# Attention over gathered neighbours: values without ones columns, one 512-column sum for both batches, and the softmax weights summed apart

## The chip, the cores and the metric

The kernel runs on one core of one Trainium2 chip. The metric is the device time in microseconds (us) of one execution. A core has five engines with queues of their own: TensorE (PE; its weight loads are shown apart as PEld), VectorE (DVE), ScalarE (ACT), GpSimd (POOL) and SyncE (SP). [...]

## The reference

Two layers over x, 8 batches of 2048 nodes with 256 features. Layer 0 is a graph convolution with two linear layers and batch norms. Layer 1, which the change concerns, is attention of each node over its neighbours in the graph, with 4 heads of 64. Both end in a residual sum and a layer norm:

```python
x = _layernorm(x + _L0_gnn_ref(x, adj, ...), axis=-1)
qkv = h @ W                                   # h is x; 256 -> 3 * 256
mask = jnp.where(adj == 0, -jnp.inf, 0.0)
scores = jnp.einsum('bhid,bhjd->bhij', q, k) / np.sqrt(HEAD_DIM) + mask
attn = jax.nn.softmax(scores, axis=-1)
out = jnp.einsum('bhij,bhjd->bhid', attn, v)
x = _layernorm(x + out, axis=-1)
```

The graph is sparse. The first nodes have many neighbours, later ones few.

## The kernel before

Layer 0 takes the first part of the span; the change leaves it as it is. Layer 1 is the function attention(). It works on pairs of batches (G2 = 2; four pairs, called passes here) and on 16 blocks of 128 nodes.

*Projection.* For each of the 8 units of a pair (a batch, and a stretch of 512 nodes) the kernel loads, norms and transposes the input and then forms keys, values and queries for 4 tiles of 128 nodes (keys_values, took_keys_values, queries, took_rows). Keys and values of a node go as one row of kv_d to DRAM, queries to q_d. A row of kv_d has 256 key columns and, for each head, 64 value columns and one column of ones, KW = 516 columns for each batch. The ones are there so that the weighted sum of a head's 65 columns gives the sum of the weights in the last one; a memset on GpSimd writes them, four at the start of each unit. Keys and values leave PSUM by two ScalarE copies (L1000, L1001).

*Block 0*, whose nodes have many neighbours, is done densely beside the projection: scores0, exps0, and weigh, which sums probabilities times the 65 columns of each head into po0 in PSUM.

*Blocks 1 to 15* use lists of neighbours. A block has ELL tiles, in which each node has its next neighbour, and CAP tiles of leftovers, in which 128 neighbours of any nodes of the block stand together. There are 132 tiles in a pass (92 and 40), 528 in all. Each tile n goes through: gather (GpSimd, L1165: 128 rows of kv_d into kg; for leftovers also query rows, L1171), score (VectorE: product pr, L1181, and its sum by heads, L1183), exps (ScalarE, L1192: the weights pw, 8 numbers a node), weigh_values (wv: values and ones times the weights, 520 columns; on VectorE, L1212, or in 8 pieces on ScalarE, L1207; for leftovers VectorE also makes the one-hot matrix oh that says which node each row belongs to, L1198), and add_up (TensorE, L1223: adds wv into the block's sum po, with the identity or with oh as the stationary operand; 260 columns, once for each batch of the pair).

The order is written out by hand. In step n of the loop stand score(n+5), exps(n+4), weigh_values(n+3), add_up of tile n-1 for the second batch and of tile n for the first, gather(n+10), then a slot of the next pair's projection (in the last pass there is none), then what was put off to this step: finish (reciprocal L1070 and product z L1072) one step after a block's last tile for the first batch and two for the second, residual (GpSimd, L1079), out_stats and later the output's norm and store.

Buffers tie the engines together: kg 10, wv 5, pw 4, pr 2, and in PSUM three banks for po (one for each batch of a block, so that a new block begins before the last one is finished), one for po0 and four for the rest. All eight banks are used.

```python
po[p, t, b] = ps_o.tile([P, NHEADS, VW], F32, name="po")
nc.tensor.matmul(
    po[p, t, b].rearrange("p h e -> p (h e)"), oh[n] if e >= 0 else ident,
    wv[n][:, b, :], start=(r == 0), stop=(r == ELL[t] + CAP[t] - 1),
)
```

Of the kernel before, what the change touches and what calls it, by code (L numbers as in the profile page):

```python
# [8 lines left out]
F32 = mybir.dt.float32  # L9
# [29 lines left out]
def tile_gcn_then_masked_attention(  # L39
# [803 lines left out]
    VW = HD + 1  # L843
    KW = D + NHEADS * VW
    inv_all = mpool.tile([P, B, NT, NHEADS], F32, name="inv_all")
# [45 lines left out]
    def attention():  # L891

        with ExitStack() as st:
            enter = st.enter_context
            ip = enter(tc.tile_pool(name="attn_in", bufs=2, side="left", reuse_waits="tile"))
            ps_o = enter(tc.tile_pool(name="ps_o", bufs=3, space=PSUM, reuse_waits="tile"))
            ps_z = enter(tc.tile_pool(name="ps_z", bufs=1, space=PSUM, reuse_waits="tile"))
            ps_m = enter(tc.tile_pool(name="ps_m", bufs=4, space=PSUM, reuse_waits="tile"))
            enter(tc.manual_schedule(engines=ALL4))

            x1, yt, x1t, ln, lo, kvr, qr, kt, q0, s0, p0, po0, zs, pms = ({} for _ in range(14))

# [58 lines left out]
            def first_queries(b):  # L961

                pm = pms["q0", b] = ps_m.tile([P, HP, P], F32, name="pm")
                for hp in range(HP):
                    for d in range(ND):
                        nc.tensor.matmul(
                            pm[:, hp, :], wq[:, d, hp * P : (hp + 1) * P], x1t[b, 0][:, d, :P],
                            start=(d == 0), stop=(d == ND - 1),
                        )
                q0[b] = ip.tile([P, HP, 2, P], F32, name="q0")  # L970
                for r in range(2):
                    nc.gpsimd.memset(q0[b][(1 - r) * HD : (2 - r) * HD, :, r, :], 0.0)
# [7 lines left out]
            def product(b, c, i, n, rhs):  # L980
# [6 lines left out]
                return pm  # L987

            def keys_values(b, c, i):
                if not i:  # L990
                    kvr[b, c] = ip.tile([P, TPC, KW], F32, name="kvr")
                    qr[b, c] = ip.tile([P, TPC, D], F32, name="qr")
                    for j in range(TPC):
                        nc.gpsimd.memset(heads(kvr[b, c][:, j, D:])[:, :, HD:], 1.0)
                pms["kv", b, c, i] = product(b, c, i, 2 * D, lambda d: wq[:, d, D:])

            def took_keys_values(b, c, i):
                pm = pms.pop(("kv", b, c, i))
                kv = kvr[b, c][:, i, :]
                nc.scalar.copy(kv[:, :D], pm[:, :D])  # L1000
                nc.scalar.copy(heads(kv[:, D:])[:, :, :HD], heads(pm[:, D:]))  # L1001

# [42 lines left out]
            def weigh(b, c, i):  # L1045
                j = c * TPC + i
                if not j:
                    po0[b] = ps_z.tile([P, NHEADS, VW], F32, name="po0")
                p = p0.pop((b, c, i))
                for h in range(NHEADS):  # L1050
                    nc.tensor.matmul(  # L1051
                        po0[b][:, h, :], p[:, h, :], heads(kvr[b, c][:, i, D:])[:, h, :],
                        start=(j == 0 and h == 0), stop=(j == NT - 1), skip_group_check=True,
                    )
# [12 lines left out]

            def finish(b, t, po):
                ri = inv_all[:, b, t, :]
                nc.vector.reciprocal(ri, po[:, :, HD])  # L1070
                z = zs[b, t] = ip.tile([P, D], F32, name="z", bufs=4)
                nc.vector.tensor_mul(  # L1072
                    heads(z), po[:, :, :HD], ri[:, :, None].to_broadcast([P, NHEADS, HD])
                )
# [24 lines left out]
            def projection(p, step):  # L1099
# [7 lines left out]
                for k, (b, c) in enumerate(units):  # L1107
# [26 lines left out]
                    if c == NCH - 1:  # L1134
                        at(u + 8, lambda b=b: finish(b, 0, po0.pop(b)))
                        at(u + 9, residual, b, 0)
                        at(u + 11, out_stats, b, 0)
# [12 lines left out]
            ON_ACT, LAST_ON_ACT = (1, 3), (0, 2, 4)  # L1150
            kg, qg, qb, oh, sc, pw, wv, po = ({} for _ in range(8))

# [23 lines left out]
            def score(n):  # L1176
                p, g = divmod(n, NG)
                t, r, col, e = tiles[g]
                q = qb[p, t] if e < 0 else qg.pop(n)
                pr = ep.tile([P, G2, D], F32, name="pr")  # L1180
                nc.vector.tensor_mul(pr, q, kg[n][:, :, :D])  # L1181
# [5 lines left out]
                sc[n] = s  # L1187

            def exps(n):
                col = tiles[n % NG][2]  # L1190
                pw[n] = ep.tile([P, G2, NHEADS], F32, name="pw", bufs=4)
                nc.scalar.activation(pw[n], sc.pop(n), AF.Exp, bias=padb[:, col : col + 1])  # L1192

            def weigh_values(n):
                e = tiles[n % NG][3]
                if e >= 0:
# [3 lines left out]
                    )  # L1200
                wv[n] = ep.tile([P, G2, NHEADS * VW], F32, name="wv", bufs=5)
                k, w = kg.pop(n), pw.pop(n)
                if n % 5 in (LAST_ON_ACT if n >= (NP - 1) * NG else ON_ACT):
                    for b in range(G2):
                        for h in range(NHEADS):
                            hs = slice(h * VW, (h + 1) * VW)
                            nc.scalar.activation(  # L1207
                                wv[n][:, b, hs], k[:, b, D:][:, hs], AF.Copy,
                                scale=w[:, b, h : h + 1],
                            )  # L1210
                    return
                nc.vector.tensor_mul(  # L1212
                    wv[n].rearrange("p b (h e) -> p b h e", e=VW),
                    k[:, :, D:].rearrange("p b (h e) -> p b h e", e=VW),
                    w[:, :, :, None].to_broadcast([P, G2, NHEADS, VW]),
                )

            def add_up(n, b):
                p, g = divmod(n, NG)
                t, r, col, e = tiles[g]  # L1220
                if not r:
                    po[p, t, b] = ps_o.tile([P, NHEADS, VW], F32, name="po")
                nc.tensor.matmul(  # L1223
                    po[p, t, b].rearrange("p h e -> p (h e)"), oh[n] if e >= 0 else ident,
                    wv[n][:, b, :], start=(r == 0), stop=(r == ELL[t] + CAP[t] - 1),
                )
                if b:
                    del wv[n]
                    oh.pop(n, None)

            def finish_block(p, t, b):
                finish(p * G2 + b, t, po.pop((p, t, b)))

# [15 lines left out]
            for n in range(NALL_G):  # L1249
# [10 lines left out]
                if n:  # L1260
                    add_up(n - 1, 1)
                add_up(n, 0)
                if n + LEAD < NALL_G:
# [3 lines left out]
                for f, args in later.pop(n, ()):  # L1267
                    f(*args)
                if r == ELL[t] + CAP[t] - 1:
                    for b in range(G2):  # L1270
                        u = n + 1 + b
                        at(u, finish_block, p, t, b)
                        at(u + 1, residual, p * G2 + b, t)
                        at(u + 3, out_stats, p * G2 + b, t)
                        if t % TPC == TPC - 1:
                            u = n + 5 + 2 * b
                            at(u, out_root, p * G2 + b, t // TPC)
# [3 lines left out]
                assert g < NG - 1 or not slots  # L1281
            add_up(NALL_G - 1, 1)
            for n in sorted(later):
# [373 lines left out]
```

## Time and profile before

| | |
|---|---|
| Median of 3 runs | 2501.35 us (2494.38 to 2505.6) |
| The profiled execution | 2506.55 us, span 2504.7 us |
| TensorE busy (8 thousand matmul records) | 2136.0 us, 85% |
| VectorE busy | 1892.7 us, 76% |
| ScalarE busy | 1248.2 us, 50% |
| GpSimd busy | 1467.8 us, 59% |
| DMA | 690.01 MB, mean 275 GB/s |
| Attention | from 1002 us to the end |

"L1223" is line 1223 of the kernel. A shape such as 128x260 is partitions by elements. A float32 matmul shows as two records, each with a weight load. The duration of a matmul record holds its pipeline's depth, so where records follow each other closely, the time of one is read from start to start. A share of busy time over the span is a mean over stages with different limits, so the attention is read in windows below.

### The profile page before, as it was taken

How to read it: one execution, taken by the hardware profiler on the slowest of the kernel's cores; microseconds unless marked ns; L12 is line 12 of the kernel's file. 1: busy time of each engine (PE TensorE's matmuls, PEld its weight loads, DVE VectorE, ACT ScalarE, POOL GpSimd, SP SyncE). 2: the span in 40 equal slices, each digit the busy share in tenths (PEclk: the TensorE clock that was granted, in tenths of full speed). 3: DMA queues.
4: the chain of work that ended last, by engine and by line, in shares of the span. 5: the costliest groups of instructions: out<-in, count | busy, mean ns of one | idle time of the engine just before them, and what ended most of it. 6: DMA issues, size and time to landing. Idle time of an engine off the chain costs nothing.

```text
span 2504.7 us, 28539 instructions
## 1 busy us (share of the span) xinstructions
PE 2136.0 (85%) x7972; PEld 1353.6 (54%) x7972; DVE 1892.7 (76%) x3650; ACT 1248.2 (50%) x3817; POOL 1467.8 (59%) x1497
## 2 busy tenths in 40 slices
PE   5998888889989999799699996899977999956554
PEld 1444443444433444577477775677765777744443
DVE  6967877776787666211788998788988889889996
ACT  6320000010103444554577775677866777767775
POOL 3405665555422876100766777577777677688874
PEclk7898999999999999899799997999998999978777
DMA  8868687685826652432988989889998899989995
GB/s 308 299 216 334 252 301 269 234 316 213 329 101 243 248 225 96 153 124 102 333 324 305 348 313 327 314 291 350 333 348 287 333 354 342 323 285 317 343 311 176
DMA packets 236153, 690.01 MB, mean 275 GB/s; under 512 B 25680, under 2 KB 91728, under 8 KB 213456
## 3 DMA queue, kind: packets, MB, share of 16 engines
q0 software_dynamic: 109248, 442.68, 49.6%
q1 hardware_dynamic: 124432, 228.62, 25.0%
q10 hardware_dynamic: 2304, 16.78, 1.7%
q8 instruction: 66, 1.08, 0.2%
q14 instruction: 103, 0.84, 0.1%
HBM read 557.19 MB, written 130.81 MB: 275 GB/s over the span
## 4 chain that ended last, share of the span: by engine, by line
PE 42%; DVE 9%; issue 6%; ACT 5%; POOL 5%; DMA 3%; another core or an unknown queue 0%; ACTq 0%; SPq 0%; DVEq 0%; POOLq 0%
PE pm L983 11%; PE po L1223 10%; PE pa L734 7%; PE pm L1032 4%; PE po L1051 4%; DVE pr L1181 3%; POOL kg L1165 2%; ACT wv L1207 2%; DMA qg<-q_d,idxq 2%; DVE s L1183 2%; PE ph L495 1%; ACT x L884 1%; DVE wv L1212 1%; PE pm L950 1%; PE pm L922 1%
## 5 line engine op out<-in xcount | busy, mean ns | idle before, releaser
L1165 POOL DMA_INDIRECT kg<-kv_d,idx x528 | 569.1, 1078 | 177.5 <-issue 104.7
L1223 PE MATMUL po<-wv,ident 128*128 128x260 f32 x1472 | 439.3, 416 | 164.5 <-DVE z L1072 58.7
L1207 ACT ACTIVATE wv<-kg,pw 128x65 f32<-128x65 f32 x1896 | 479.1, 338 | 28.2 <-issue 14.5
L1223 PEld LDWEIGHTS po<-wv,ident 128*128 128x128 f32 x1472 | 288.4, 207 | 254.1 <-issue 123.0
L1183 DVE TENSOR_REDUCE s<-pr 128x8 f32<-128x512 f32 x528 | 362.1, 686 | 34.6 <-ACT pw L1192 0.3
L983 PE MATMUL pm<-wq,x1t 128*128 128x512 f32 (+1 forms) x1024 | 376.7, 492 | 1.5 <-issue 1.5
L642 PE MATMUL pa<-e,wt 128*128 128x512 f32 x648 | 310.4, 627 | 33.8 <-DVE e L350 31.4
L1181 DVE TENSOR_TENSOR pr<-qb,kg 128x512 f32<-128x512 f32 x368 | 255.3, 694 | 10.9 <-DMA kg<-kv_d,idx 9.6
L1212 DVE TENSOR_TENSOR wv<-kg,pw 128x520 f32<-128x520 f32 x291 | 212.2, 729 | 58.3 <-PE po L1223 18.8
L1192 ACT ACTIVATE pw<-s,padb 128x8 f32<-128x8 f32 x528 | 156.8, 300 | 170.4 <-DVE s L1183 122.3
L983 PEld LDWEIGHTS pm<-wq,x1t 128*128 128x128 f32 x1024 | 188.3, 192 | 84.6 <-issue 70.0
L642 PEld LDWEIGHTS pa<-e,wt 128*128 128x128 f32 x648 | 126.8, 202 | 183.7 <-issue 145.1
L1223 PE MATMUL po<-wv,oh 128*128 128x260 f32 x640 | 210.3, 428 | 11.5 <-DVE wv L1212 6.1
L560 POOL DMA_INDIRECT e<-xs_d,idx x116 | 127.2, 1097 | 120.3 <-PE pa L642 54.6
L1171 POOL DMA_INDIRECT qg<-q_d,idxq x160 | 164.1, 1026 | 48.8 <-issue 48.1
L1079 POOL TENSOR_TENSOR x<-z,x 128x256 f32<-128x256 f32 x128 | 121.2, 949 | 106.6 <-DVE z L1072 91.6
L1223 PEld LDWEIGHTS po<-wv,oh 128*128 128x128 f32 x640 | 133.4, 216 | 45.4 <-issue 10.0
L309 POOL DMA_INDIRECT av<-in_adj_dram,fidx x116 | 128.9, 1112 | 48.7 <-issue 27.8
L371 ACT COPY e<-ph 128x512 f32<-128x512 f32 x32 | 18.8, 586 | 273.1 <-PE ph L366 272.8
L1051 PEld LDWEIGHTS po<-kvr,p 128*128 128x128 f32 x1024 | 138.4, 198 | 10.7 <-issue 3.8
L1032 PE MATMUL pm<-q,kt 128*128 128x256 f32 x512 | 136.6, 390 | 4.7 <-issue 3.3
L928 DVE TENSOR_TENSOR x<-pm,x 128x512 f32<-128x512 f32 x64 | 43.9, 686 | 125.3 <-PE pm L922 121.7
(202 smaller groups left out, 3714.3 us busy)
## 6 DMA issues: line engine op xcount, KB each, us to landing
kv_d<-kvr SPq DMA_DIRECT2D x32, 1032.0 KB
e<-h_d SPq DMA_DIRECT2D x28, 1024.0 KB
e<-in_adj_dram SPq DMA_DIRECT2D x16, 1024.0 KB
xt<-in_x_dram SPq DMA_DIRECT2D x16, 1024.0 KB
xs_d<-xt ACTq DMA_DIRECT2D x16, 1024.0 KB
y_d<-y SPq DMA_DIRECT2D x32, 512.0 KB
yt<-y_d SPq DMA_DIRECT2D x32, 512.0 KB
x<-in_x_dram SPq DMA_DIRECT2D x32, 512.0 KB
```

What stands on the lines that cost most here:

```text
L642: nc.tensor.matmul(pa[:, c, :], w, xg[n].t[:, c * CH : (c + 1) * CH], start=(k == 0), stop=(k == count - 1),)
L734: nc.tensor.matmul(py, w[:, f, :], t[:, f, :], start=(f == 0), stop=(f == 1))
L983: nc.tensor.matmul(pm, x1t[b, c][:, d, i * P : (i + 1) * P], rhs(d), start=(d == 0), stop=(d == ND - 1),)
L1032: nc.tensor.matmul(pm[:, hp].rearrange("p r q -> p (r q)"), k[:, hp, :], q0[b][:, hp].rearrange("p r q -> p (r q)"), start=False, stop=Tru ...
L1051: nc.tensor.matmul(po0[b][:, h, :], p[:, h, :], heads(kvr[b, c][:, i, D:])[:, h, :], start=(j == 0 and h == 0), stop=(j == NT - 1), skip_g ...
L1165: nc.gpsimd.indirect_dma_start(out=kg[n].rearrange("p b e -> p (b e)"), out_offset=None, in_=kv_d[p][:], in_offset=bass.IndirectOffsetOnAx ...
L1171: nc.gpsimd.indirect_dma_start(out=qg[n].rearrange("p b e -> p (b e)"), out_offset=None, in_=q_d[p][:], in_offset=bass.IndirectOffsetOnAxi ...
L1181: nc.vector.tensor_mul(pr, q, kg[n][:, :, :D])
L1183: nc.vector.tensor_reduce(s.rearrange("p b h -> p (b h)"), pr.rearrange("p b (h e) -> p (b h) e", e=HD), AX.X, ALU.add,)
L1207: nc.scalar.activation(wv[n][:, b, hs], k[:, b, D:][:, hs], AF.Copy, scale=w[:, b, h : h + 1],)
L1212: nc.vector.tensor_mul(wv[n].rearrange("p b (h e) -> p b h e", e=VW), k[:, :, D:].rearrange("p b (h e) -> p b h e", e=VW), w[:, :, :, None ...
L1223: nc.tensor.matmul(po[p, t, b].rearrange("p h e -> p (h e)"), oh[n] if e >= 0 else ident, wv[n][:, b, :], start=(r == 0), stop=(r == ELL[t ...
```

## The change

The values lose their columns of ones: a row of kv_d has 2 x 256 = 512 columns for each batch. Keys and values leave PSUM in one 512-column copy. Block 0 still needs the ones; it gets a small tile v1 of its own, with three buffers, made for each tile of nodes by a memset and a second copy of the values (ones_and).

In the lists, wv has 512 columns, both batches, and add_up sums them in one product a tile into one PSUM bank (po, two banks). The sum of the weights is formed apart: the weights of a block are kept in one tile pw (three buffers), VectorE sums the columns of the ELL tiles (tensor_reduce in finish_block), and for the leftovers TensorE sums them with an 8-column product with oh as the stationary operand (add_weights, into pe, one PSUM bank). finish_block now takes both batches at once, two steps after a block's last tile, and the steps behind it move accordingly. The buffers of pr go from 2 to 1 and of q0 from 2 to 1.

```diff
-    KW = D + NHEADS * VW
+    KW = 2 * D
...
-            ps_o = enter(tc.tile_pool(name="ps_o", bufs=3, space=PSUM, reuse_waits="tile"))
+            ps_o = enter(tc.tile_pool(name="ps_o", bufs=2, space=PSUM, reuse_waits="tile"))
+            ps_s = enter(tc.tile_pool(name="ps_s", bufs=1, space=PSUM, reuse_waits="tile"))
...
-                q0[b] = ip.tile([P, HP, 2, P], F32, name="q0")
+                q0[b] = ip.tile([P, HP, 2, P], F32, name="q0", bufs=1)
...
+            def ones_and(b, c, i, values):
+                v = v1[b, c, i] = ip.tile([P, NHEADS, VW], F32, name="v1", bufs=3)
+                nc.gpsimd.memset(v[:, :, HD:], 1.0)
+                nc.scalar.copy(v[:, :, :HD], heads(values))
...
-                kv = kvr[b, c][:, i, :]
-                nc.scalar.copy(kv[:, :D], pm[:, :D])
-                nc.scalar.copy(heads(kv[:, D:])[:, :, :HD], heads(pm[:, D:]))
+                nc.scalar.copy(kvr[b, c][:, i, :], pm)
+                ones_and(b, c, i, pm[:, D:])
...
-                pr = ep.tile([P, G2, D], F32, name="pr")
+                pr = ep.tile([P, G2, D], F32, name="pr", bufs=1)
...
+                if not r:
+                    pw[p, t] = ep.tile([P, MAXT, G2, NHEADS], F32, name="pw", bufs=3)
...
-            def add_up(n, b):
+            def add_up(n):
...
                 nc.tensor.matmul(
-                    po[p, t, b].rearrange("p h e -> p (h e)"), oh[n] if e >= 0 else ident,
-                    wv[n][:, b, :], start=(r == 0), stop=(r == ELL[t] + CAP[t] - 1),
+                    po[p, t].rearrange("p b e -> p (b e)"), oh[n] if e >= 0 else ident,
+                    wv.pop(n).rearrange("p b e -> p (b e)"),
+                    start=(r == 0), stop=(r == ELL[t] + CAP[t] - 1),
                 )
+            def add_weights(n):
...
+                if e == edge0[t]:
+                    pe[p, t] = ps_s.tile([P, G2, NHEADS], F32, name="pe")
+                nc.tensor.matmul(
+                    pe[p, t].rearrange("p b h -> p (b h)"), oh.pop(n),
+                    weights_of(n).rearrange("p b h -> p (b h)"),
+                    start=(e == edge0[t]), stop=(e == edge0[t] + CAP[t] - 1),
+                )
+            def finish_block(p, t):
+                sums = ep.tile([P, G2, NHEADS], F32, name="sums")
+                nc.vector.tensor_reduce(
+                    sums.rearrange("p b h -> p (b h)"),
+                    pw.pop((p, t))[:, : ELL[t]].rearrange("p r b h -> p (b h) r"), AX.X, ALU.add,
+                )
+                nc.vector.tensor_add(sums, sums, pe.pop((p, t)))
+                ri = inv_all[:, p * G2 : (p + 1) * G2, t, :]
+                nc.vector.reciprocal(ri, sums)
+                z = ip.tile([P, G2, D], F32, name="z")
+                nc.vector.tensor_mul(
...
                 if n:
-                    add_up(n - 1, 1)
-                add_up(n, 0)
+                    add_weights(n - 1)
+                add_up(n)
...
+                    at(n + 2, finish_block, p, t)
                     for b in range(G2):
-                        u = n + 1 + b
-                        at(u, finish_block, p, t, b)
-                        at(u + 1, residual, p * G2 + b, t)
-                        at(u + 3, out_stats, p * G2 + b, t)
+                        at(n + 3, residual, p * G2 + b, t)
+                        at(n + 5 + b, out_stats, p * G2 + b, t)
                         if t % TPC == TPC - 1:
-                            u = n + 5 + 2 * b
+                            u = n + 7 + 2 * b
```

## The prediction

> **What bounds the kernel now.** I read first the table of windows, for the stages; then who waited for whom in each window, engine by engine; then the timeline of TensorE and of VectorE. The change touches only the attention, 1002 us to the end. From 1002 to about 1195 the first projection runs alone. Then 528 gather tiles go through four passes of 132; in the first three the next pair's projection is threaded in, in the last none. The table of windows (busy us and count for PE, weight load, DVE, ACT, POOL; clock, DMA share, GB/s), windows cut inside the passes:
>
> ```profile
> 1230.00:1540.00 310.00, 283.00 (x1346) 218.14 (x1344) 269.45 (x558) 220.71 (x756) 218.39 (x245) 0.98 0.90 325
> 1540.00:1870.00 330.00, 302.51 (x1402) 233.67 (x1403) 283.40 (x587) 233.47 (x798) 229.84 (x263) 0.94 0.90 323
> 1870.00:2190.00 320.00, 288.95 (x1363) 221.56 (x1362) 280.37 (x582) 230.47 (x785) 232.61 (x264) 0.96 0.91 325
> 2190.00:2485.00 295.00, 178.31 (x568) 131.60 (x567) 262.98 (x515) 208.40 (x818) 227.33 (x222) 0.78 0.88 302
> ```
>
> By the count of score sums (L1183: 122, 128, 127, 136) a tile takes 2.54, 2.58, 2.52 and 2.17 us. In the first three windows TensorE and VectorE are both near 90% busy; in the last TensorE is far below and VectorE is the bound. In the first three, who waits (second window, VectorE, then TensorE; total us, times, longest):
>
> ```profile
> DVE wv L1212 <- PE po L1223: 9.8, 5, 4.5
> DVE x L928 <- PE pm L922: 6.5, 6, 3.0
> DVE pr L1181 <- DMA kg<-kv_d,idx: 1.4, 2, 0.8
> ```
> ```profile
> PE po L1223 <- DVE inv_all L1070: 7.0, 1, 7.0
> PE po L1223 <- DVE z L1072: 5.3, 2, 3.8
> ```
>
> So the two engines stall each other, and the gathers, 0.9 of the DMA share, are hardly waited for. Between stalls TensorE runs without a gap, each start where the row before hands over (start, us, operation):
>
> ```profile
> 1403.98 1.04 PE L1223 MATMUL po<-wv,ident 128*128 128x260 f32 x4
> 1404.86 0.38 PE L1014 MATMUL pm<-ident,kvr 128*128 128x128 f32 x2
> ...
> 1407.75 1.00 PE L1051 MATMUL po<-kvr,p 128*128 128x65 f32 x8
> 1408.59 0.38 PE L1026 MATMUL pm<-bias,ident 128*128 128x512 bf16 x1
> 1408.81 1.03 PE L1032 MATMUL pm<-q,kt 128*128 128x256 f32 x4
> 1409.67 1.88 PE L983 MATMUL pm<-wq,x1t 128*128 128x512 f32 x4
> 1411.38 0.60 PE L1223 MATMUL po<-wv,oh 128*128 128x260 f32 x2
> ```
>
> Start to start: two 260-column sums 0.88 us; four 65-column products (8 records) 0.84, so 0.105 a record; two 512-column products 1.71, so 0.855 each. VectorE in the last pass, the same way:
>
> ```profile
> 2300.44 0.69 DVE L1183 TENSOR_REDUCE s<-pr 128x8 f32<-128x512 f32 x1
> 2301.04 0.17 DVE L1070 RECIPROCAL inv_all<-po 128x4 f32<-128x4 f32 x1
> 2301.25 0.42 DVE L1072 TENSOR_TENSOR z<-po,inv_all 128x256 f32<-128x256 f32 x1
> 2301.59 0.68 DVE L1181 TENSOR_TENSOR pr<-qb,kg 128x512 f32<-128x512 f32 x1
> ```
>
> A reciprocal holds the queue 0.21 us, the 256-wide product 0.34, a score sum 0.60.
>
> **What the Trainium skill says.** "TensorE: Matmul & The Clock Gate", LDWEIGHTS: a load costs the columns over 1.2 GHz, 107 ns for 128; the trace agrees where the product is too short to hide it (0.105 us a record in the 65-column products). The same page, the HAM clock gate: idle beyond a window of about 3.4 us halves the clock. The trace shows 0.94 and 0.78 where TensorE waits most, so a stall there costs more than its length. "VectorE: DVE Perf Modes", The DRAIN you can't avoid: a semaphore between two VectorE operations costs nothing extra; the trace nearly agrees: 0.17 us of reciprocal, then the waiting product 0.21 after its start.
>
> **Part by part.** Sums against the profiled execution (2504.7 us span, 2506.55 in all, 5.2 above the median 2501.35); the result is then put on the median.
>
> TensorE, per pass. Each tile has one 512-column sum for two of 260: 0.88 to 0.855, so 132 x 0.025 = 3.3 us off. Each leftover tile (40 a pass) gains an 8-column product (add_weights) with the one-hot matrix as stationary operand. Its matmuls hide no load, so one of its two loads and the next sum's first lie bare: 2 x 0.105 = 0.21, 8.4 a pass. Not shown in the trace; from one bare load (0.105) to the price of a whole 260-column product (0.44), I take 0.21. Net +5.1 a pass, 15.3 in the three passes where TensorE is short; in the last it is hidden by VectorE.
>
> VectorE, per block (15 a pass). Before: twice reciprocal and product, 2 x 0.55 = 1.10. After: a reduce over up to 9 tiles' weights (at most 72 elements; L825 with 48 takes 0.20, with its wait 0.24), an add from PSUM 0.21, a reciprocal 0.21, a 512-wide product from PSUM, like L928's 0.69 and so 0.60 in the queue: 1.26. +0.16, 2.4 a pass (reduce 0.17 to 0.35: 1.4 to 4). With one pr buffer the product waits for the previous score sum. That bites where the sum stands directly before it, in the built order 18, 19, 18 and 32 times: the start goes from 0.60 to about 0.73, and the sum after it follows after 0.72 in place of 0.79: +0.06, 1.1 a pass and 1.9 in the last (0 to 0.13 each). wv loses 8 of 520 elements: under 0.01 x 79. Together +2.7 a pass, +3.8 in the last, where all of it is on the path.
>
> ScalarE. The copy of keys goes from 0.37 to a 512-wide 0.58, the value copy stays: +0.21 x 32 = 6.8 a pass, at a 70% share. The ones (128 memsets, as before) now come per tile, and the value copy waits for its memset on GpSimd, behind gathers and residual adds; queued behind that copy are the score exponentials. I take +1 a pass for both. If that cover is gone, see the fourth case. In the first projection v1's third-last buffer is freed by the product one slot earlier or at the head of the same slot; ScalarE waits for that slot's queries anyway: nothing (0 to +3).
>
> GpSimd and SP. No issue is added: gathers, stores and loads keep their places; q0's single buffer makes its memset wait for the last scores of the batch before, twice a pass, and behind it stands only a gather whose tile is used ten later. Rows fall from 4128 to 4096 bytes, 0.8%. "DMA: Bandwidth & Descriptors", How a descriptor splits into AXI transactions, says pieces begin at 256-byte boundaries; 4096-byte rows stay on them, 4128-byte ones don't. No run shows the price; VectorE's waits for kg and qg add up to some 14 us in the four windows, which bounds the gain; I take none.
>
> Waits that move. VectorE's weighted values reuse a buffer freed by the second batch's sum, one tile late; now by the one sum: a tile more of slack. Their waits for TensorE make 12.3, 13.2 and 8.1 us in the three windows; a third goes: -11. What is late next there is the norm (L928), which still wants a transpose of the slot before, 16 times a pass. In the other direction the wait only changes its name: the old sum of a new block's tile n+1, second batch, waited for finish at n+1. Now the sums have two banks, but the weights' bank (pe) is single: the first leftover product of the new block waits for finish at n+2. It is the second tile in 10 of 15 blocks, so it stands at n+3: the same lead of one tile. In 5 blocks it comes a tile or more later. No gain taken.
>
> Sum: TensorE 15.3, VectorE half of 3 x 2.7 = 4, ScalarE 3, last pass 3.8, relief -11: +15. 2506.55 + 15 = 2521.6; on the median 2516.
>
> **Rivals.** Measured differences under 0.5% (12.5 us) I count as no change.
> *Decoupling wins (faster).* One mechanism: the extra tile of slack between VectorE and TensorE. Place: the three threaded passes. Price: two thirds of the 33.6 us above and half of TensorE's 31 us of waits for z and inv_all (6.5, 12.3, 12.2) go, -38; costs at half weight (7.7 + 4 + 2) and the last pass 3.8 give +17: -21, 2480. It decides when TensorE's stalls fall short enough to keep the clock near 1. For it: both engines under 95% busy, so some 9% is stall. Against: norm and pe keep a lead of one.
> *Costs and relief cancel.* Half the TensorE cost lies in its idle time and a little of its waits goes too: 17 - 11 - 4 = +2, 2503.
> *Values wait for ones.* GpSimd waits for VectorE 47 us (residual adds) and 40 us (L139) in the three windows. If half of that reaches the value copy and half again TensorE: +22 on top of 15, 2538. It decides when GpSimd comes to the memset later than ScalarE's spare 30% covers. Against: no wait of ScalarE for GpSimd's memsets shows today.
>
> **Numbers.** Forecast 0.38 (its own range 2508 to 2526), decoupling 0.27, cancel 0.22, ones 0.13. Nearly all of the first and all of the last lie beyond 0.5%: slower 0.49; same 0.24; faster 0.27. Range 2474 to 2552: down past decoupling's centre, up past the ones case with the 8-column product at its dear end (+0.23 x 120 = 28 us at half weight, 14).
>
> **What would show it.** Tiles take 2.56 to 2.60 us in threaded passes and 2.20 in the last; L1253's records in start-to-start 0.2 us; PE pe <- DVE sums in place of PE po <- DVE z; wv's waits for PE shorter. Wrong if threaded tiles fall to 2.48 with a clock of 0.98 or more, or if ScalarE's value copy waits for a memset in tens of us.

## The result, and the profile after

The changed kernel takes 2511.18 us (median of 20 runs, 2505.05 to 2526.47) beside 2502.39 us for the kernel before on the same chip (20 runs, 2494.38 to 2513.08): ratio 1.0037, interval 1.0022 to 1.0052, some 9 us slower. The forecast said 2516, slower by 15. The difference is under the 0.5% that the prediction counted as no change, so its sign rests on the interval alone. The profiled execution took 2524.3 us (span 2522.6).

Table of windows of the changed kernel, the same stretches and columns as before (busy us and count for PE, weight load, DVE, ACT, POOL; clock, DMA share, GB/s):

```profile
1230.00:1540.00 310.00, 286.11 (x1186) 178.59 (x1186) 273.26 (x553) 229.37 (x768) 215.32 (x246) 0.99 0.88 324
1540.00:1870.00 330.00, 307.05 (x1224) 189.21 (x1224) 293.32 (x596) 240.61 (x804) 235.01 (x268) 0.96 0.89 322
1870.00:2190.00 320.00, 294.11 (x1172) 180.87 (x1173) 286.09 (x585) 235.28 (x782) 236.25 (x266) 0.95 0.89 320
2190.00:2485.00 295.00, 190.52 (x385) 77.77 (x384) 262.26 (x503) 203.64 (x805) 225.98 (x223) 0.79 0.89 310
```

In the first three windows VectorE is busy 852.7 us of 960; it was 833.2. So VectorE does 19 us more in the same time, some 7 of them because these windows hold 378 tiles in place of 375. TensorE's busy time rises from 874.5 to 887.3. Both engines carry more, and in these two executions both wait less. By the count of score sums (123, 129, 126, 135) a tile takes 2.52, 2.56, 2.54 and 2.19 us; before, by the same count of starts (121, 128, 126, 136), it took 2.56, 2.58, 2.54 and 2.17. (The prediction counted 122 and 127 in the first and third, with sums that reach over the window's edge.)

Windows shift against the work, so I cut the attention by tiles instead, from the start of one score sum to that of another. Each number is of one profiled execution:

| us | before | after |
|---|---|---|
| first score sum starts | 1196.6 | 1206.9 |
| tiles 1 to 396 (three passes with a projection) | 1004.2 | 1006.6 |
| the rest, to the last score sum | 278.9 | 281.7 |
| from there to the end of the span | 25.0 | 27.3 |
| first score sum to end | 1308.1 | 1315.7 |

The 10 us ahead of the first score sum do not belong to the change: the first store of the projection already stands at 1036.0 and 1046.0 us, and over the profiles of this study the first score sum starts anywhere between 1193 and 1207. The attention itself takes 7.6 us longer, close to the measured 8.8. That closeness shows little. One execution differs from the next by more than these rows do: the kernel before with one pr buffer (b_pr1 below) was profiled in an execution 15 us under its median, and there tiles 1 to 396 took 988.6 us. The rows tell where to look; the comparisons of medians below tell what counts.

Where it went, on VectorE. Its timeline in the last pass of the changed kernel (start, us, operation), a product pr that waits for the score sum before it, and a block's end:

```profile
2315.26 0.69 DVE L1189 TENSOR_REDUCE s<-pr 128x8 f32<-128x512 f32 x1
2315.98 0.69 DVE L1187 TENSOR_TENSOR pr<-qb,kg 128x512 f32<-128x512 f32 x1
...
2317.98 0.26 DVE L1261 TENSOR_REDUCE sums<-pw 128x8 f32<-128x64 f32 x1
2318.28 0.16 DVE L1265 TENSOR_TENSOR sums<-sums,pe 128x8 f32<-128x8 f32 x1
2318.47 0.20 DVE L1267 RECIPROCAL inv_all<-sums 128x8 f32<-128x8 f32 x1
2318.71 0.69 DVE L1269 TENSOR_TENSOR z<-po,inv_all 128x512 f32<-128x512 f32 x1
2319.32 0.68 DVE L1187 TENSOR_TENSOR pr<-qg,kg 128x512 f32<-128x512 f32 x1
```

Read starts, not durations. From the score sum to pr is 0.72; with a free buffer it was 0.60. From the reduce to the next pr is 1.34; the median over the blocks is 1.33 (0.28, 0.20, 0.24, 0.61), where before it was 1.10. In the three threaded passes that makes 45 x 0.23 + 55 x 0.12 = 17 us more work, and in the last pass 15 x 0.23 + 32 x 0.12 = 7. Against it, VectorE's waits over tiles 1 to 396 fall from 98.2 to 81.9 us, and in the last pass from 17.7 to 12.6. Work less waits gives +1 and +2 us, beside the +2.4 and +2.8 of the table. The fall of 16 us is itself of the size by which executions differ: in b_pr1's profile the kernel before, with one pr buffer, has 77.8 us of these waits.

Who VectorE waits for now, second window of the changed kernel (total us, times, longest):

```profile
DVE wv L1228 <- ACT pw L1205: 8.4, 5, 2.5
DVE lo_st L868 <- POOL x L1084: 3.8, 1, 3.8
DVE x L929 <- PE pm L923: 3.5, 3, 1.8
```

The line of before that stood on top, wv waiting for TensorE's po, is gone. Over the three passes wv's waits for TensorE fall from 33.5 to 8.1 us; those of the norm rise from 14.3 to 20.7, those of wv for ScalarE from 10.8 to 15.7, and a new one, the output's statistics waiting for GpSimd's residual add, takes 13.5 (1.2 before). The fall of wv's waits and the new wait are more than the accident of one execution. For wv the kernel before has 33.5 us, and 26.7 with one pr buffer (b_pr1); the changed kernel and its variants with as many wv buffers have 13.4 at most. The statistics wait 0.6 to 1.2 us in the three profiles of the kernel before and its variants, and 7 us or more in all eleven of the changed kernel and its own.

TensorE's waits in the same window:

```profile
PE pe L1253 <- DVE sums L1265: 11.2, 2, 10.7
```

With 2.3 us that the view puts down to the reduce (L1261) it is 13.5; it was 12.3 for inv_all and z there. Over the three passes: 33.1 for the sums in place of 35.3 for z and inv_all. TensorE's timeline in the first pass:

```profile
1409.65 0.28 PE L1253 MATMUL pe<-pw,oh 128*128 128x8 f32 x2
1409.79 1.10 PE L1239 MATMUL po<-wv,ident 128*128 128x512 f32 x2
1410.73 0.38 PE L1029 MATMUL pm<-bias,ident 128*128 128x512 bf16 x1
...
1412.67 1.02 PE L1239 MATMUL po<-wv,ident 128*128 128x512 f32 x2
1413.53 0.38 PE L1017 MATMUL pm<-ident,kvr 128*128 128x128 f32 x2
```

A 512-column sum takes 0.86 from start to start (1412.67 to 1413.53). Behind an 8-column product it takes 0.94, and the product itself 0.14: together 0.22 for each leftover tile.

The tail: from TensorE's last sums, first before, then in the changed kernel (in brackets the idle time before, and its releaser):

```profile
2481.06 1.20 PE L1223 MATMUL po<-wv,ident 128*128 128x260 f32 x2 [4.57 <-DVE z L1072]
...
2483.79 3.59 PE L1223 MATMUL po<-wv,ident 128*128 128x260 f32 x8
2487.22 1.04 PE L1223 MATMUL po<-wv,oh 128*128 128x260 f32 x4
```
```profile
2497.19 0.57 PE L1253 MATMUL pe<-pw,oh 128*128 128x8 f32 x2 [3.85 <-DVE sums L1265]
2497.61 3.76 PE L1239 MATMUL po<-wv,ident 128*128 128x512 f32 x4
2501.16 1.92 PE L1239 MATMUL po<-wv,oh 128*128 128x512 f32 x2
```

In both kernels TensorE has stood for some 4 us, and the sums that follow run at half speed: 0.43 us a record of 260 columns where it was 0.22 in the first pass, and 0.89 a record of 512 where it was 0.43. The granted clock is 0.50 in both (2481 to 2487 us before, 2497 to 2503 after). So this is no difference: from the start of the last score sum to the end of TensorE's last sum it is 9.5 us before and 9.3 after. The 2.3 us of the table come later. From the start of the kernel's last VectorE operation to the end of the span it is 9.3 us before and 11.3 after, and the last store is issued equally soon, 1.2 us into it. The kernel before and its variants have 9.2 to 9.5 us there in three profiles, the changed kernel and its variants 11.3 to 12.7 in eleven. What these closing 2 us are, no run shows.

### The profile page after: what moved, and what is told of

Same layout as the page of the kernel before. It is cut to its first block, busy times and chain, and to the rows that moved or that the text cites. A ratio compares the mean times of both kernels' runs of the same rounds, so it can differ in the third digit from the quotient of the medians.

```text
span 2522.6 us, 27141 instructions
## 1 busy us (share of the span) xinstructions
PE 2173.1 (86%) x7236; PEld 1172.2 (46%) x7236; DVE 1911.9 (76%) x3650; ACT 1268.9 (50%) x3817; POOL 1467.7 (58%) x1497
## 4 chain that ended last, share of the span: by engine, by line
PE 39%; DVE 12%; ACT 6%; issue 6%; DMA 5%; POOL 3%; SPq 0%; another core or an unknown queue 0%; DVEq 0%; POOLq 0%; ACTq 0%
PE pm L984 10%; PE po L1239 8%; PE pa L734 7%; DVE pr L1187 4%; PE po L1054 3%; PE pm L1035 3%; ACT wv L1223 2%; DMA kg<-kv_d,idx 2%; DVE s L1189 2%; DVE wv L1228 2%; ACT x L884 2%; POOL kg L1171 1%; PE ph L495 1%; DMA kv_d<-kvr 1%; PE pm L923 1%
## 5 line engine op out<-in xcount | busy, mean ns | idle before, releaser
L1223 ACT ACTIVATE wv<-kg,pw 128x64 f32<-128x64 f32 x1896 | 476.3, 338 | 4.7 <-remote 2.4
L1239 PE MATMUL po<-wv,ident 128*128 128x512 f32 x736 | 435.3, 689 | 32.3 <-DVE s L1189 14.5
L642 PE MATMUL pa<-e,wt 128*128 128x512 f32 x648 | 319.9, 643 | 35.6 <-DVE e L350 28.6
L1228 DVE TENSOR_TENSOR wv<-kg,pw 128x512 f32<-128x512 f32 x291 | 209.0, 718 | 25.8 <-ACT pw L1205 14.6
L1239 PE MATMUL po<-wv,oh 128*128 128x512 f32 x320 | 181.9, 652 | 21.3 <-DVE wv L1228 6.0
L1239 PEld LDWEIGHTS po<-wv,ident 128*128 128x128 f32 x736 | 134.1, 214 | 101.4 <-issue 46.3
L1054 PEld LDWEIGHTS po<-v,p 128*128 128x128 f32 x1024 | 136.0, 195 | 52.5 <-issue 50.7
L1253 PE MATMUL pe<-pw,oh 128*128 128x8 f32 x320 | 54.0, 241 | 107.2 <-DVE sums L1265 75.0
L1084 POOL TENSOR_TENSOR x<-z,x 128x256 f32<-128x256 f32 x128 | 112.3, 896 | 58.2 <-DVE z L1269 42.8
L1253 PEld LDWEIGHTS pe<-pw,oh 128*128 128x128 f32 x320 | 63.3, 218 | 159.3 <-issue 108.5
```

The lines of the kernel that those rows point to most:

```text
L642: nc.tensor.matmul(pa[:, c, :], w, xg[n].t[:, c * CH : (c + 1) * CH], start=(k == 0), stop=(k == count - 1),)
L1054: nc.tensor.matmul(po0[b][:, h, :], p[:, h, :], v[:, h, :], start=(j == 0 and h == 0), stop=(j == NT - 1), skip_group_check=True,)
L1223: nc.scalar.activation(v[:, b, hs], k[:, b, D:][:, hs], AF.Copy, scale=w[:, b, h : h + 1],)
L1228: nc.vector.tensor_mul(v.rearrange("p b (h e) -> p b h e", e=HD), k[:, :, D:].rearrange("p b (h e) -> p b h e", e=HD), w[:, :, :, None].to ...
L1239: nc.tensor.matmul(po[p, t].rearrange("p b e -> p (b e)"), oh[n] if e >= 0 else ident, wv.pop(n).rearrange("p b e -> p (b e)"), start=(r = ...
```

## The experiments

Ratios are to the kernel before, measured in the same batch on the same chip; 0.001 is 2.5 us. The changed kernel has its 1.0037 from its own comparison and was not run beside these kernels, so a difference from it takes that ratio over to another batch and carries both intervals, 0.002 to 0.0025 together (5 to 6 us). a_noaw, a_wv4, b_wv6 and a_pr2 shared one chip, b_pr1, a_nored, a_pad and a_lean another, and a_bare, a_early, a_hoist and a_later a third. Some kernels need room in SBUF for one more buffer; there `ok`, a tile used only at the very end, is put into another tile's buffers.

**What the 8-column products cost** (a_noaw)

```diff
-                if e == edge0[t]:
-                    pe[p, t] = ps_s.tile([P, G2, NHEADS], F32, name="pe")
-                nc.tensor.matmul(
-                    pe[p, t].rearrange("p b h -> p (b h)"), oh.pop(n),
-                    weights_of(n).rearrange("p b h -> p (b h)"),
-                    start=(e == edge0[t]), stop=(e == edge0[t] + CAP[t] - 1),
-                )
+                oh.pop(n)
...
-                nc.vector.tensor_add(sums, sums, pe.pop((p, t)))
+                nc.vector.tensor_add(
+                    sums, sums, ones[:, : G2 * NHEADS].rearrange("p (b h) -> p b h", b=G2)
+                )
```

> The changed kernel without the 8-column products: the leftover tiles' weights are left out of the sums, and the add in finish takes a constant in place of them; all else stays. Theory: the products cost TensorE 0.22 us each, 120 of them in the threaded passes (26 us, about half of it on the path), and hold TensorE at the end of the last pass. The time falls by 10 to 16 us below the changed kernel, to a ratio of 0.997 to 1.000 against before. Rival (the loss is VectorE's alone, TensorE has room): within 4 us of the changed kernel, ratio 1.002 to 1.004.

Measured: 2505.82 us, 1.0003 (0.9988 to 1.0017), about 8.5 us below the changed kernel. That lies between the two, nearer the theory. The products take 0.22 x 120 = 26 us of TensorE's time in the three passes; a third of it shows (8.5 with an error of 5). TensorE's waits, second window of this kernel, suggest the reason:

```profile
PE po L1239 <- DVE wv L1228: 11.1, 5, 4.3
```

With no pe to wait for, TensorE waits for VectorE all the same, 11.1 us where it waited 11.2 for the sums. The tail falls to 23.9 us from 27.3: TensorE's last sum ends 5.6 us after the last score sum starts, not 9.3, so in the changed kernel the wait in the tail is of this product's making. In these two profiles 3.4 of the 8.5 us lie there; that leaves some 5 for the 26 us in the three passes.

**Is it wv's slack? One buffer less in the changed kernel, one more in the one before** (a_wv4, b_wv6)

```diff
-                wv[n] = ep.tile([P, G2, D], F32, name="wv", bufs=5)
+                wv[n] = ep.tile([P, G2, D], F32, name="wv", bufs=4)
```

> The changed kernel with 4 buffers of weighted values in place of 5, so that VectorE again needs the sum of one tile back as before the change. Theory (the extra tile of slack gives back some 10 us): 8 to 12 us slower than the changed kernel, ratio 1.007 to 1.009 against before. Rival (the slack is worth nothing, the costs were simply hidden): no change, ratio 1.003 to 1.005.

```diff
-                wv[n] = ep.tile([P, G2, NHEADS * VW], F32, name="wv", bufs=5)
+                wv[n] = ep.tile([P, G2, NHEADS * VW], F32, name="wv", bufs=6)
```

> The kernel before with 6 buffers of weighted values in place of 5 (a tile used once at the end shares another's buffer to make room): the slack of the change alone, without its costs. Theory: 6 to 12 us faster than before, ratio 0.995 to 0.998. Rival (slack is worth nothing): 0.999 to 1.001.

Measured: with one buffer less 2519.17, 1.0052 (1.0032 to 1.0072), 4 us above the changed kernel with an error of 6: nearer the rival, but the theory's 8 lies within the error, and wv's waits for TensorE come back to 17 us of the 33.5 only. With one more in the kernel before 2511.98, 1.0028 (1.0015 to 1.0041), slower by 7 us. The slack did what it was to do: wv's waits for TensorE fall from 33.5 to 4.9 us over the three passes. But nothing was won. VectorE's waits of this kernel in the second window:

```profile
DVE x L928 <- PE pm L922: 13.6, 7, 5.6
DVE wv L1212 <- ACT pw L1192: 4.9, 4, 2.2
DVE inv_all L1070 <- PE po L1223: 4.0, 5, 1.9
```

The norm took 6.5 in the kernel before, and inv_all waited for TensorE 2.7 us over all three passes; now it is 16.5 over them, and the norm 22.6. VectorE hardly waits for the weighted values any longer and comes too early to the next thing that stands one step behind TensorE. The theory fell for the kernel before: slack at wv alone wins nothing there. Why it loses 7 us is open; VectorE's waits add up to 101.8 us over the three passes, beside 98.2. In the changed kernel finish stands a step later too, and the lists' inv_all waits for TensorE no more.

**What the single pr buffer costs** (a_pr2: two buffers in the changed kernel; b_pr1: one in the kernel before)

```diff
-                pr = ep.tile([P, G2, D], F32, name="pr", bufs=1)
+                pr = ep.tile([P, G2, D], F32, name="pr")
```

> The changed kernel with two buffers of pr again (a tile used once at the end shares another's buffer to make room). 87 products no longer wait for the score sum before them. Theory from the trace after, 0.12 us each and 10 us in all, 3.8 of them in the last pass where VectorE is the bound: 5 to 8 us faster than the changed kernel, ratio 1.0005 to 1.0015 against before. As predicted (0.06 each): 2 to 4 us. Rival (the wait is hidden): within 2 us, ratio 1.003 to 1.0045.

> The kernel before with one buffer of pr in place of two: the self wait alone. 71 products stand directly behind a score sum. Theory from the trace after (0.12 us each): 8.5 us on VectorE, 3.0 of it in the last pass, so 4 to 8 us slower than before, ratio 1.0015 to 1.003. As predicted (0.06): 2 to 4 us, 1.001 to 1.0015. Rival (hidden): 0.9995 to 1.0005.

Measured: a_pr2 2508.47, 1.0006 (0.9991 to 1.0022), 7.7 us below the changed kernel. b_pr1 2504.32, 1.0008 (0.9990 to 1.0026), 2 us above before, which may be nothing. In the timeline of a_pr2 the step is short again:

```profile
2323.79 0.69 DVE L1189 TENSOR_REDUCE s<-pr 128x8 f32<-128x512 f32 x1
2324.39 0.68 DVE L1187 TENSOR_TENSOR pr<-qb,kg 128x512 f32<-128x512 f32 x1
```

0.60 in place of 0.72, the median of 87 places in the one kernel and in the other. That is 10 us of VectorE's time; in the kernel before the same wait stands at 71 places, 8.5 us. Of these 8 and 2 show, with errors of 5 and 4.5. The first meets the theory; the second does not part the theory from no cost at all.

**What the reduce costs** (a_nored: the sum is the first list tile's weights and pe)

```diff
-                nc.vector.tensor_reduce(
-                    sums.rearrange("p b h -> p (b h)"),
-                    pw.pop((p, t))[:, : ELL[t]].rearrange("p r b h -> p (b h) r"), AX.X, ALU.add,
-                )
-                nc.vector.tensor_add(sums, sums, pe.pop((p, t)))
+                nc.vector.tensor_add(sums, pw.pop((p, t))[:, 0], pe.pop((p, t)))
```

> The changed kernel without the reduce over a block's list tiles: the sums take the first tile's weights and the leftovers only, so the other list tiles' weights are left out. VectorE loses 0.28 us a block, 17 us in 60 blocks. Theory (VectorE's share counts in full in the last pass, about half in the threaded ones): 4 + 6 = 10 us faster than the changed kernel, ratio 0.9985 to 1.001 against before. Rival (TensorE bounds the threaded passes, VectorE counts only in the last): 4 us faster, ratio 1.0015 to 1.003.

Measured: 2507.42, 1.0014 (0.9996 to 1.0032), 5.8 us below the changed kernel (error 6), between the two. The reduce held VectorE 60 x 0.28 = 17 us; a third shows, with an error as large as what shows.

**Do rows of 4096 bytes help the gathers?** (a_pad: 516 columns for each batch again, the four added ones zero)

```diff
-    KW = 2 * D
+    KW = 2 * D + NHEADS
...
+                    nc.gpsimd.memset(kvr[b, c][:, :, 2 * D :], 0.0)
...
```

> The changed kernel with rows of 516 columns a batch in DRAM again, the last 4 unused: row size and alignment of before, with the rest of the change. Theory (the gathers are not waited for): within 3 us of the changed kernel, ratio 1.0025 to 1.005. Rival (4096-byte rows move faster and part of the relief is theirs): 5 us or more slower than the changed kernel, 1.0055 or more. Other rival (4096-byte rows cost, as the longer wait at the ends of passes suggests): 5 us or more faster, 1.002 or less.

Measured: 2514.74, 1.0052 (1.0034 to 1.0070), some 4 us above the changed kernel, with an error of 6. That lies between the theory and the first rival and parts neither; the second rival, that the shorter rows cost, falls. This kernel has a memset on GpSimd more for each unit, too. VectorE's waits for gathered rows give no sign of a price: 7.2 us over the three passes here, 10.1 in the changed kernel.

**All three costs away at once** (a_bare: two pr buffers, no products, no reduce; pr and the products as in the edits above, and in finish_block)

```diff
...
-                nc.vector.tensor_add(sums, sums, pe.pop((p, t)))
+                nc.vector.tensor_add(
+                    sums, pw.pop((p, t))[:, 0], ones[:, : G2 * NHEADS].rearrange("p (b h) -> p b h", b=G2)
+                )
```

> The changed kernel with pr in two buffers, without the 8-column products and without the reduce: the sum of the weights is the first list tile's weights plus a constant. Theory (the three costs stand beside each other and add: 8.5 for the products, 7.7 for pr, 5.8 for the reduce, as measured one at a time, against a kernel at about 1.0044): 22 us below the changed kernel, ratio to before 0.993 to 0.998; the rest, 11 us or so below before, is what the one 512-column sum and its slack bring. Rival (the costs hide behind each other, since TensorE and VectorE stall each other by turns, and the slack brings nothing): ratio 0.999 to 1.002.

Measured: 2462.24 beside 2471.09 for the kernel before, 0.9967 (0.9957 to 0.9977): 8 us below before, and 17.5 below the changed kernel's ratio (1.0037; the expectation's 1.0044 was set too high). One at a time they gave 8.5 + 7.7 + 5.8 = 22. So within their errors the costs add, and the rival, that they hide behind each other, falls. What is left of the change without them is a gain of about 8 us, on this chip. The loss of products and reduce does not lean on another chip's ratio: a_early (next), which has both and two pr buffers and differs otherwise in the step of its sums alone, was measured beside it at 1.0006, some 10 us more (error 3.5). TensorE's waits over tiles 1 to 396 of this kernel:

```profile
PE po L1239 <- DVE wv L1228: 47.4, 14, 14.5
PE pm L951 <- ACT x L884: 17.0, 30, 5.3
```

Next to nothing is left of TensorE's waits for sums or z; it now waits for VectorE's values, and VectorE not for wv's buffers at all.

**Sums one step earlier** (a_early: reduce and add at n+1, reciprocal and z at n+2; two pr buffers)

```diff
-            def finish_block(p, t):
-                sums = ep.tile([P, G2, NHEADS], F32, name="sums")
+            def sum_weights(p, t):
+                sums = sm[p, t] = ep.tile([P, G2, NHEADS], F32, name="sums")
...
+            def finish_block(p, t):
+                sums = sm.pop((p, t))
...
+                    at(n + 1, sum_weights, p, t)
                     at(n + 2, finish_block, p, t)
```

> The changed kernel with pr in two buffers (its ratio to before was 1.0006), and reduce and add one step earlier (n+1, so that the single bank pe is free a tile sooner); reciprocal and z stay at n+2. Theory (TensorE's 33 us of waits for the sums in the threaded passes hold the time): half of them go, 5 to 12 us faster than with pr alone, ratio 0.996 to 0.999. Rival (the wait moves: VectorE now waits for the last leftover product of the tile just before, and TensorE for z): 0.9995 to 1.003, with a wait of VectorE for PE at the add of over 15 us.

Measured: 2473.12, 1.0006 (0.9997 to 1.0016), the ratio that two pr buffers alone (a_pr2) had on another chip. TensorE's waits over tiles 1 to 396:

```profile
PE pe L1253 <- DVE sums L1265: 24.9, 5, 8.2
PE po L1239 <- DVE wv L1228: 24.0, 7, 14.7
```

The waits for sums are fewer, five, but long, and as many microseconds are waits for wv. A wait of VectorE at the add, which the rival wanted, doesn't show. As far as waits tell, TensorE waits because VectorE is late, whichever of its results happens to be next. By the ratio the theory fell; with a_pr2 not run on this chip this is not shown.

**A lean variant that lost** (a_lean, and its two parts a_hoist and a_later; all with two pr buffers)

```diff
+            vs = [ip.tile([P, NHEADS, VW], F32, name=f"v1_{j}", bufs=1) for j in range(3)]
+            for v in vs:
+                nc.gpsimd.memset(v[:, :, HD:], 1.0)
...
-                v = v1[b, c, i] = ip.tile([P, NHEADS, VW], F32, name="v1", bufs=3)
-                nc.gpsimd.memset(v[:, :, HD:], 1.0)
+                v = v1[b, c, i] = vs[((b * NCH + c) * TPC + i) % 3]
...
-                        at(n + 5 + b, out_stats, p * G2 + b, t)
+                        at(n + 6 + b, out_stats, p * G2 + b, t)
...
-                            u = n + 7 + 2 * b
+                            u = n + 8 + 2 * b
```

> The changed kernel with two buffers of pr, the ones of v1 written once at the start instead of once a tile, and the output's statistics one step later, since VectorE now waits 13.5 us for the residual adds in the threaded passes (lo_st <- POOL x). Theory: 7 us from pr, 3 to 6 from the statistics, 0 to 2 from the ones: 10 to 15 below the changed kernel, ratio 0.998 to 1.000 against before. Rival (the waits for the residual only change their name): as with two buffers of pr alone, 1.0000 to 1.0015.

> The changed kernel with pr in two buffers and the ones of v1 written once, into three fixed tiles, in place of 128 memsets. It is one of the two parts of the kernel that came out at 1.0082. Theory (the ones in the middle of GpSimd's queue cost nothing; fixed tiles cost nothing): 0.999 to 1.002, as with pr alone. Rival (the hoist is what slowed that kernel): 1.005 to 1.010.

> The changed kernel with pr in two buffers and the statistics of the output one step later (n+6+b in place of n+5+b, the norm behind it one step later too). The other part of the kernel at 1.0082. Theory (the later statistics put ScalarE's or VectorE's small operations where the scores stand, and slowed that kernel): 1.005 to 1.010. Rival (it was the hoisted ones): 0.999 to 1.002.

Measured: both parts 2526.03, 1.0082 (1.0052 to 1.0112), where two pr buffers alone gave 1.0006: the theory fell by some 19 us. The ones alone (a_hoist, down to `% 3]`) 2480.92, 1.0051 (1.0033 to 1.0069); the statistics alone (a_later, the rest) 2483.79, 1.0055 (1.0037 to 1.0073). So each part seems to cost some 11 us, and the two together about what they add up to; on the third chip, next to a_early at 1.0006, they are slower by 8 and 11 us. Neither has a wait in its profile that would explain it, and the statistics' wait for the residual add, which the later step was to spare, stays: 9.8 us in a_later, beside 9.0 in a_pr2. Why both lose is open, and so is whether two pr buffers alone would have kept their 1.0006 on the third chip.

The profile of a_lean shows one thing more. Two successive lines of its timeline with all engines:

```profile
1316.20 0.95 POOL L1180 DMA_INDIRECT qg<-q_d,idxq  x1 [0.30 <-issue]
1318.91 0.60 ACT L1046 ACTIVATE p<-pm 128x512 f32<-128x512 f32 x1 [6.56 <-remote]
```

ScalarE stands 6.56 us for something that the profile can't name ("remote"), and from 1317.2 to 1318.9 no engine starts an instruction. Five such waits of this line make 26.6 us. They are no sufficient cause. The kernel before has 21.9 us of "remote" waits on ScalarE in the same passes; and on the third chip, where no kernel has any, both parts of this variant lose all the same.

## Why the prediction was right, and where its sum was off

The likeliest case came out: slower, by less than forecast, with the costs above the relief. Term by term:

- **Price of the 8-column product.** 0.21 forecast, 0.22 seen. The sum held; its halves, 0.105 each by the forecast, came as 0.14 for the product and 0.08 for the sum behind it.
- **TensorE, 15.3 charged in full.** This is the term that was mis-sized. Of the 26 us that the products take, 8.5 (error 5) reach the end, and 3.4 of these seem to lie in the tail, where the forecast had the products hidden. The step that failed is "15.3 in the three passes where TensorE is short": busy near 90% in a window did not make it the bound there. It waits some 90 us for VectorE and ScalarE in those passes, and a_noaw and a_bare show that without the products it waits for VectorE still.
- **VectorE, 4 + 3.8.** The block's end costs 0.23 more, not 0.16: the reduce holds the queue 0.28 where 0.24 was reckoned, and the reciprocal, now of 8 columns, 0.24 where it was 0.21. The self wait of pr costs 0.12, not 0.06: the forecast had the score sum behind a waiting pr follow after 0.72 in place of 0.79, and it doesn't (median 0.80). So the work grew by 17 + 7 us where 8 + 4 was forecast. Taken out by themselves, pr's buffer gave 7.7 and the reduce 5.8, so by these figures, each with an error of 5 to 6, more of the loss is here than forecast, and less on TensorE.
- **Relief, -11.** wv's waits for TensorE fell by 25 us, more than the third forecast; the norm took over 6 of it, as forecast, and the residual's wait 13.5, which was not. VectorE's waits fell by 16 in all between the two profiles, which is no more than executions differ. The mechanism was misread in part: wv's slack alone doesn't bring the gain (b_wv6 has it and is slower). As far as the waits tell, a block's sum must also be wanted a step later, with finish; no run moves finish alone, so this is argued, not shown. What remains without the three costs, -8 on the third chip, holds this relief and the shorter sum together, and the runs don't part them.
- **The wait that changes its name.** 35.3 us for z and inv_all became 33.1 for the sums. Right, and so was taking no gain for it.
- **ScalarE, +3.** The copy of both takes 0.58 where the keys took 0.37, as reckoned; wv's waits for ScalarE rose by 5 us between the two profiles. No run took it alone.
- **First projection and tail, nothing.** The projection takes 145.2 and 145.4 us from its first to its last store of keys and values, so nothing. The tail grew by 2.3, which the sum didn't have, but in the closing instructions and not in the sums. These run at half speed in both kernels. The clock gate that the prediction cited (the Trainium skill, "TensorE: Matmul & The Clock Gate", The HAM clock gate) puts the clock at half after an idle window of about 3.4 us; here the clock is 0.50 with 4.57 and 3.85 us idle ahead, so the trace agrees, and the two kernels pay alike.
- **DMA, no gain.** a_pad agrees within its error, but can't exclude a few us.
- **Rivals.** Decoupling did not win: of the 65 us of waits that it wanted to shorten 41 are left, and tiles 1 to 396 take 2.54 us each, as before. (The main forecast's sign, 2.56 to 2.60, did not come either; its 2.20 for the last pass nearly did, with 2.19.) Cancelling is nearer than the chance of 0.22 suggests: 9 us lie midway between its 2 and the forecast's 15. No ScalarE wait for a memset of the ones shows in the passes, so the fourth case falls; yet taking the memsets out made things worse, and that isn't understood.

The two errors, too much on TensorE and too little on VectorE, went in opposite directions, and the nearness of 2516 to 2511 owes something to that luck.

No kernel here that computes the whole beats the one before beyond its interval: a_pr2 and a_early, at 1.0006, come level with it.

## What to carry to other kernels

Where two engines at 90% each stall the other by turns, neither is the bound by itself: a cost added to either showed here by a fifth to three quarters of its size, with errors that are often as large, and a wait removed on one came back at the next operation that stands one step behind the other. So in such a stage read an engine's added work together with what its waits become, and ask of a new slack what else is wanted just as early. Price short operations on VectorE that form a chain from start to start, with their waits. A buffer taken away from a pair that alternates is a wait wherever the two stand back to back. And before a few us between two profiles are read as the work of a change, look how far two executions of one kernel lie apart.

## What the runs showed of the hardware that was not expected

- The Trainium skill, "VectorE: DVE Perf Modes", The DRAIN you can't avoid, reports eight copies that took as long with a semaphore after each as with one at the end: the semaphore costs nothing extra there. Here a product that waits for the score sum before it starts 0.72 us after that sum's start, one that doesn't wait 0.60 (a_pr2), and an add whose result the next operation needs holds the queue 0.20. In a_early, where the next one does not need it, it holds the queue 0.08, as the timeline below shows. The measurement decides for these operations: such a wait costs 0.12 us.
- The same kernel before took 2502 to 2505 us in three comparisons and 2471 in the one on the third chip. In the ten profiles from the first three, ScalarE has 39 to 59 us of waits in the three passes for which the profile names nothing or "remote"; in the four of the third chip it has none. The start is no quicker there: the first score sum stands at 1198 to 1202 us, beside 1193 to 1207. What these waits are, no run shows.

VectorE's timeline in a_early, the add and what follows it:

```profile
2326.53 0.16 DVE L1265 TENSOR_TENSOR sums<-sums,pe 128x8 f32<-128x8 f32 x1
2326.61 0.69 DVE L1187 TENSOR_TENSOR pr<-qg,kg 128x512 f32<-128x512 f32 x1
```
